# Selective-scan hybrid network: the order of VectorE's product with C and the next side step in a unit

## The chip, the cores and the metric

The kernel runs on one NeuronCore of a Trainium2 chip. The metric is device time in microseconds (us) of one execution, the median of several runs. The engines are named as in the profile: PE (TensorE, matrix multiplications), DVE (VectorE), ACT (ScalarE), POOL (GpSimd), SP (SyncE, which here only issues DMAs).

## The reference

The input is an image batch x of shape (4, 96, 64, 64). Four layers follow each other: a selective scan over the image in four directions (layer 0), a convolution block (layer 1), a spectral block with a feed-forward part (layer 2), and an attention product with a feed-forward part (layer 3). The change touches only the scan of layer 0. Cut to it, for each image and each of the four directions k:

```
xs     = the image's 192 channels after convolution and SiLU, as a sequence of 4096 places
B, C   = 16 values each per place;  delta = softplus(...) per channel and place
h[l]   = exp(delta[l] * A) * h[l-1] + (delta[l] * xs[l]) * B[l]       # 192 channels x 16 states
y[l]   = sum over the 16 states of h[l] * C[l]
```

The y of the four directions are turned back, added, normalised over the channels and multiplied by a weight. The output has the input's shape.

## The kernel before, in words

**Units.** One batch image, one direction and one stretch of 1024 places make a step. A step has 24 units: each holds 32 channels x 4 states on 128 partitions, with 1024 places along the free axis. There are 1536 units in all. `scans` runs them one after the other in an order written out by hand; the compiler's scheduler does not reorder its instructions (it stands under `manual_schedule`). One turn of its loop is a slot.

**What one unit issues**, with the lines of the profile:

- `inputs` (L1280, POOL): w = (delta * x) * B, two slots ahead.
- `decays` (L1287, ACT): da = exp(delta * A) into a pair of PSUM banks, one slot ahead. There are two such pairs, so the decay of unit s+2 goes into the banks that unit s has used. Just before it, `keep` (L1315, ACT) copies the last state of unit s for the step that follows it.
- `states` (L1303, DVE): the scan. If the unit's product goes to POOL, the scan writes over w in SBUF; if it goes to DVE, the scan writes over da in PSUM.
- `product` (L1318): w = h * C, either on DVE, issued right behind the scan, or on POOL, issued two slots later. `share` decides which, from a running estimate of how far DVE is ahead of POOL: 860 products go to DVE and 676 to POOL.
- `sums` (L1341, PE): the sum over the states by matmuls into `ps_y`, three slots behind the second unit of a pair.

**Side work.** All other layers run beside the scan. Each is a generator that yields one small step at a time with its engine and an estimated time: `pe(...)`, `ac(...)` or `dv(...)`. At the end of each slot the loop calls `advance` until a budget (`owed`) is spent or nothing fits. A step that changes the engine is, as a rule, only taken in a later slot than the step before it. A DVE step adds its estimated time to `beside[0]`, which is then added to `ahead_by[0]`, the estimate that `share` reads. So DVE's queue holds, slot by slot: the scan, its product if it is DVE's, and the DVE side steps of that slot.

DVE side steps that this text names: L633 and L636 (the softplus of delta and the product delta * x; L636 reads what L633 wrote), L755 and L757 (output normalisation and residual), L849 (residual of the convolution block), L894, L896 and L912 (layer norm and a cast of layers 2 and 3).

**Buffers.** Four tiles each of delta, delta * x, B and C, eight of w; their loads are issued by SP at fixed units of a step.

The end of a slot, before:

```
            if x is not None:
                states(x)
            for group in due.get(slot, ()):
                sums(group)
            ...
            while owed > 0.0:
                did = advance(stages)
                if did is None:
                    break
                owed -= did
                ahead_by[0] += beside[0]
                beside[0] = 0.0
```

Of the kernel before, what the change touches and what calls it, by code (L numbers as in the profile page):

```python
# [97 lines left out]
def hybrid_kernel(ctx: ExitStack, tc: tile.TileContext, a: dict):  # L98
# [4 lines left out]
    nc = tc.nc  # L103
# [352 lines left out]
    def flush():  # L456
        while to_store:
            out, t, then = to_store.pop(0)
            store(out, t)
            if then is not None:  # L460
                then()
# [763 lines left out]
    def plan():  # L1225

        stats = (group_norm(b, arriving(b)) for b in range(1, B))
        out = [Stage("weights", 2, later_weights(), *stats)] + front(1) + front(2)
        out += middle(0) + layers_2_and_3(0) + front(3)
        for b in (1, 2):  # L1230
            out += middle(b) + layers_2_and_3(b)
        return out

    def scans(stages):
# [22 lines left out]
        def fetch(step, name, i):  # L1257
            t = step[name][i] = wide(name)
            if name in "BC":
                lo = 4 * i + (NS if name == "C" else 0)  # L1260
                of = d_bc[step["k"]][step["b"] % 3][step["c"], lo : lo + 4].unsqueeze(0)
            else:
                of = (d_delta if name == "d" else d_du)[step["k"]][step["b"] % 3]
                of = of[step["c"], 32 * i : 32 * i + 32].unsqueeze(1)
            load(t, of.to_broadcast([32, 4, CH2]))

        def need(step):

            while not traced[step["b"]].issuperset((step["k"] % 2, 2 * step["c"] + e) for e in (0, 1)):
                force(stages)  # L1270
            flush()
# [6 lines left out]
        def inputs(x):  # L1278
            x["w"] = wide("w")
            nc.gpsimd.tensor_mul(x["w"], x["step"]["g"][x["i"]], x["step"]["B"][x["j"]])  # L1280

        def decays(x, last):
            if last is not None:
                keep(last)
            av = (x["step"]["k"] * NI + x["i"]) * NJ + x["j"]
            x["da"] = decay_banks()
            act(x["da"], x["step"]["d"][x["i"]], AF.Exp, scale=aneg[:, av : av + 1])  # L1287

        def share(x):

            on_vector, on_pool = PRODUCT_US
            lead = ahead_by[0] + SCAN_US - on_pool
            x["pool"] = abs(lead - on_pool) < abs(lead + on_vector)
            lead += -on_pool if x["pool"] else on_vector
            ahead_by[0] = max(-AHEAD, min(lead, AHEAD))

        def states(x):
            step, u = x["step"], x["u"]
            share(x)
            order = slice(None, None, -1) if step["k"] >= 2 else slice(None)  # L1300
            x["h"] = x["w"] if x["pool"] else x["da"]
            start = 0.0 if step["n"] == 0 else steps[x["number"] - 1]["last"][:, u : u + 1]
            nc.vector.tensor_tensor_scan(  # L1303
                x["h"][:, order], x["da"][:, order], x["w"][:, order], start, ALU.mult, ALU.add
            )
            if not x["pool"]:
                product(x, nc.vector)

        def keep(x):
            step, u = x["step"], x["u"]  # L1310
# [6 lines left out]
        def product(x, engine):  # L1317
            x["made"] = engine.tensor_mul(x["w"], x["h"], x["step"]["C"][x["j"]])  # L1318
# [12 lines left out]
        def sums(group):  # L1331
            step, first, last = group[0]["step"], group[0]["j"] == 0, group[0]["j"] == NJ - 1
            if first:
                step["y"] = bank("y")
            y = step["y"]

            made = None
            for m in (1, 0):
                for e in (1, 0):
                    q = 2 * e + m  # L1340
                    done = mm(y[32 * q : 32 * q + 32], lhsT=const("stack"), rhs=group[m]["w"][:, e * CH : e * CH + CH],  # L1341
                              start=first, stop=last)
                    if made is None:
                        made = group[0]["made"]
                        tc.add_manual_dep(done.ins, made.ins.name, mybir.DependencyInfo(
                            mybir.DependencyClass.Sync, mybir.DependencyReason.DATA), reason="sums")
            if last:
                summed.append((group, y))

        def sums_out():  # L1350
            while summed:
                group, y = summed.pop(0)
                step = group[0]["step"]
                yt = sp.tile([128, CH], F32, name="yt", bufs=1)
                nc.scalar.copy(yt, y)
                which = group[0]["pass"]
                for e in (0, 1):
                    to = d_y[step["k"]][step["b"] % 2][2 * step["c"] + e]
                    later(to[64 * which : 64 * which + 64], yt[64 * e : 64 * e + 64],
                          (lambda b=step["b"]: through(b)) if which == len(PASSES) - 1 and e == 1 else None)  # L1360

        owed = 0.0
        stages += plan()
        behind = middle(B - 1)
        stages += behind
# [7 lines left out]
        for slot in range(len(units) + 6):  # L1373
            clock[0] = slot
            x = units[slot] if slot < len(units) else None
            if x is not None:
                if x["u"] == 0:


                    last = len(units) - NST * PC  # L1380
                    if slot < last:
                        rate = max(RATE, sum(s.work for s in stages if s not in behind) / (last - slot))
                    else:
                        rate = sum(s.work for s in stages) / (len(units) - slot)
                for name, i in OWN.get(x["u"], ()):
                    fetch(x["step"], name, i)
                if x["number"] + 1 < len(steps) and x["u"] in LOADS:
                    if x["u"] == 14:
                        need(steps[x["number"] + 1])
                    for name, i in LOADS[x["u"]]:  # L1390
                        fetch(steps[x["number"] + 1], name, i)
            flush()
            if slot + 1 < len(units):
                decays(units[slot + 1], units[slot - 1] if slot > 0 else None)
            sums_out()
            if slot + 2 < len(units):
                inputs(units[slot + 2])
            if 2 <= slot < len(units) + 2 and units[slot - 2]["pool"]:
                product(units[slot - 2], nc.gpsimd)
# [4 lines that stand above are left out]
            for e, (us, most) in SHARE.items():  # L1404
                room[e] = min(room[e] + us, most)
            tensor[0] = 0.0
            held_banks[0] -= freed[0]
            freed[0] = 0
            owed = min(owed + rate, 8.0)
            while owed > 0.0:  # L1410
                did = advance(stages)
                if did is None:
                    break
                owed -= did
                ahead_by[0] += beside[0]
                beside[0] = 0.0
        flush()


    clock, tensor = [-1], [0.0]  # L1420
    beside, ahead_by = [0.0], [0.0]
# [45 lines left out]
    def advance(stages):  # L1467

        while stages and not stages[0].fill():
            stages.pop(0)  # L1470
        if stages:
            banks_left = BANKS["mm"] - held_banks[0]
            for stream in stages[0].active:
                engine, us, banks, _ = stream["next"]
                if banks and banks > banks_left:

                    banks_left = 0
                elif fits(stream):
                    if engine != "wait":
                        room[engine] -= us  # L1480
                    if engine == "pe":
                        tensor[0] += us
                    if engine == "dve":
                        beside[0] += us
                    return stages[0].step(stream)
        return None
# [21 lines left out]
    with tc.manual_schedule(engines={nc.tensor.engine, nc.scalar.engine, nc.vector.engine, nc.gpsimd.engine, nc.sync.engine}):  # L1508
        scans(stages)
# [153 lines left out]
```

## Time and profile before

| what | value |
|---|---|
| median of 3 runs | 6039.0 us (6030.13 to 6051.08) |
| the profiled execution | 6029.4 us; span of its instructions 6027.6 us |
| granted PE clock in it, mean | 0.857 |
| busy: DVE / POOL / ACT / PE | 88% / 86% / 64% / 76% of the span |
| scans on DVE (L1303) | 1536, about 2.34 us each |
| products with C on DVE (L1318) | 860, 1.225 us each |
| products with C on POOL (L1318) | 676, 2.375 us each |
| decays on ACT (L1287) | 1536, 1.116 us each |
| last scan starts / last product on DVE starts | 5545.7 / 5544.6 us |

How to read the lines: a group line gives the source line, the engine, the operation, output <- inputs, the shapes and the count; then the busy time in us and the mean of one in ns; then the idle time of the engine just before these instructions and what ended most of it. A wait line gives who waited for whom, with the total in us, the number of times and the longest. A timeline line gives start and duration in us. The scan phase runs from about 100 us to 5548 us; after it only the last image's layers 1 to 3 remain.

### The profile page before, as it was taken

The numbers are of one execution on the slowest core, as the hardware profiler recorded it, in microseconds if no ns is written. First come the engines' busy times: TensorE is split into PE (matmuls) and PEld (weight loads), VectorE is DVE, ScalarE is ACT, GpSimd is POOL, SyncE is SP. The second block draws the span as 40 slices with busy tenths as digits, with TensorE's granted clock in tenths as the row PEclk, the third lists the DMA queues.
The fourth block names the chain that finished last, engine by engine and source line by source line (L and its number), as shares of the span: only waits on it lengthen the run. The fifth ranks groups of instructions, "written<-read, shape, count | busy, mean of one in ns | idle before, by whom it ended". The sixth has DMA issues, their size and how long they took to land. (4 is left out here: it accounts for less than half of the span.)

```text
span 6027.6 us, 78329 instructions
## 1 busy us (share of the span) xinstructions
PE 4564.8 (76%) x27668; PEld 1682.2 (28%) x27668; DVE 5280.0 (88%) x3583; ACT 3856.1 (64%) x6056; POOL 5154.5 (86%) x2219
## 2 busy tenths in 40 slices
PE   6743867755898776686568888768888877779998
PEld 2100212211222642121012246211222642112284
DVE  4999898899999899989999999999999999897045
ACT  4853776764665677877556657777666677665335
POOL 4987898999999999989999999999999999897000
PEclk9855978877999888797689989878999888789999
DMA  5654575667754654466776446557754664674101
GB/s 182 229 177 152 195 227 183 219 211 232 216 161 148 200 194 154 159 196 205 229 238 186 164 159 217 166 175 224 220 173 155 199 199 144 184 239 146 48 16 38
DMA packets 425084, 1078.44 MB, mean 179 GB/s; under 512 B 79378, under 2 KB 81268, under 8 KB 423540
## 3 DMA queue, kind: packets, MB, share of 16 engines
q1 hardware_dynamic: 424692, 1073.44, 56.0%
q8 instruction: 219, 3.59, 0.3%
q14 instruction: 173, 1.42, 0.1%
HBM read 857.02 MB, written 220.66 MB: 179 GB/s over the span
## 5 line engine op out<-in xcount | busy, mean ns | idle before, releaser
L1280 POOL TENSOR_TENSOR scan_w<-scan_g,scan_B 128x1024 f32<-128x1024 f32 x1536 | 3606.5, 2376 | 242.0 <-PE ps_y L1341 112.3
L1287 ACT ACTIVATE ps_da<-scan_d,aneg 128x1024 f32<-128x1024 f32 x1536 | 1714.4, 1116 | 324.3 <-DVE scan_w L1318 176.1
L1318 POOL TENSOR_TENSOR scan_w<-scan_w,scan_C 128x1024 f32<-128x1024 f32 x676 | 1605.4, 2375 | 153.3 <-ACT state L1315 102.4
L1303 DVE TENSOR_TENSOR_SCAN ps_da<-ps_da,state,scan_w 128x1024 f32<-128x1024 f32 x633 | 1483.0, 2343 | 103.8 <-ACT ps_da L1287 92.5
L1341 PE MATMUL ps_y<-scan_w,cst 128*32 128x512 f32 x6144 | 1003.0, 730 | 590.8 <-POOL scan_w L1318 297.8
L1303 DVE TENSOR_TENSOR_SCAN scan_w<-ps_da,state,scan_w 128x1024 f32<-128x1024 f32 x519 | 1214.2, 2341 | 32.9 <-ACT ps_da L1287 30.7
L1318 DVE TENSOR_TENSOR scan_w<-ps_da,scan_C 128x1024 f32<-128x1024 f32 x860 | 1053.1, 1225 | 71.7 <-DMA scan_C<-bc 6.4
L1303 DVE TENSOR_TENSOR_SCAN ps_da<-ps_da,scan_w 128x1024 f32<-128x1024 f32 x227 | 518.4, 2284 | 58.3 <-ACT ps_da L1287 51.1
L1341 PEld LDWEIGHTS ps_y<-scan_w,cst 128*32 128x32 f32 x6144 | 147.2, 117 | 1221.5 <-POOL scan_w L1318 505.1
L1315 ACT COPY state<-ps_da 128x1 f32<-128x1 f32 x654 | 104.1, 159 | 488.4 <-DVE scan_w L1318 486.5
L829 PE MATMUL ps_mm<-h,wd 128*32 128x512 f32 x3144 | 363.5, 593 | 7.0 <-ACT r L169 7.0
L1303 DVE TENSOR_TENSOR_SCAN scan_w<-ps_da,scan_w 128x1024 f32<-128x1024 f32 x157 | 357.8, 2279 | 9.5 <-ACT ps_da L1287 6.9
L567 PE MATMUL ps_mm<-xp,taps 128*128 128x512 f32 x576 | 285.9, 639 | 51.6 <-ACT xp L547 22.2
L806 PE MATMUL ps_mm<-wd,w 128*32 128x512 f32 x1944 | 243.1, 613 | 17.9 <-ACT h L810 8.7
L618 PE MATMUL ps_mm<-xd,dtw 128*128 128x512 f32 x256 | 165.4, 737 | 70.8 <-ACT z L640 43.8
L1315 ACT COPY state<-scan_w 128x1 f32<-128x1 f32 x498 | 93.2, 187 | 192.0 <-DVE scan_w L1303 191.6
L627 ACT ACTIVATE z<-ps_mm 128x512 f32<-128x512 f32 x192 | 114.4, 596 | 148.3 <-PE ps_mm L622 76.5
L633 DVE SCALAR_TENSOR_TENSOR ps_mm<-ps_mm,z 128x512 f32<-128x512 f32 x192 | 131.3, 684 | 87.7 <-ACT z L631 82.6
L888 PE MATMUL ps_mm<-r,cst 128*128 128x512 f32 x220 | 149.4, 768 | 62.4 <-ACT r L885 13.8
L672 PE MATMUL ps_mm<-ya,cst 128*64 128x512 f32 x192 | 183.2, 1043 | 9.1 <-ACT acc L912 8.6
L810 ACT ACTIVATE h<-ps_mm 128x512 f32<-128x512 f32 x258 | 150.6, 596 | 53.8 <-PE ps_mm L806 50.9
L829 PEld LDWEIGHTS ps_mm<-h,wd 128*32 128x32 f32 x3144 | 110.6, 109 | 239.8 <-issue 207.3
(360 smaller groups left out, 6536.9 us busy)
## 6 DMA issues: line engine op xcount, KB each, us to landing
scan_g<-du SPq DMA_DIRECT2D x384, 512.0 KB, 5.0
scan_d<-delta SPq DMA_DIRECT2D x384, 512.0 KB, 5.9
scan_B<-bc SPq DMA_DIRECT2D x256, 512.0 KB, 5.3
scan_C<-bc SPq DMA_DIRECT2D x256, 512.0 KB, 5.2
y<-yt SPq DMA_DIRECT2D x384, 128.0 KB, 2.7
du<-g SPq DMA_DIRECT2D x128, 256.0 KB, 3.0
delta<-z SPq DMA_DIRECT2D x128, 256.0 KB, 2.8
tab<-in_etab SPq DMA_DIRECT2D x112, 256.0 KB, 4.0
```

The source lines that it names most:

```text
L567: mm(p, lhsT=taps[:, t, 0:128], rhs=window(t, c + e), start=t == 0, stop=t == 8)
L618: mm(p, lhsT=dtw[:, o + 2 * third, 0:128], rhs=xd, start=True, stop=True)
L672: mm(split(p[:64]), lhsT=const("two")[:, :64], rhs=t[:, :L].rearrange("p (w h) -> p h w", h=H)[:, c * RPC : (c + 1) * RPC, :], start=True, ...
L806: mm(p[32 * n : 32 * n + 32], lhsT=w1[:, 32 * g : 32 * g + 32], rhs=xin[:, n : n + 15 : 2, 1 : W + 1], start=True, stop=True)
L810: act(h[:, :, 1 : W + 1], split(p), AF.Relu)
L829: mm(p[32 * n : 32 * n + 32], lhsT=held["wd"][:, groups[i], o, dx, :], rhs=here[i][:, :, dx : dx + W], start=dx == 0, stop=dx == 2)
L1280: nc.gpsimd.tensor_mul(x["w"], x["step"]["g"][x["i"]], x["step"]["B"][x["j"]])
L1287: act(x["da"], x["step"]["d"][x["i"]], AF.Exp, scale=aneg[:, av : av + 1])
L1303: nc.vector.tensor_tensor_scan(x["h"][:, order], x["da"][:, order], x["w"][:, order], start, ALU.mult, ALU.add)
L1315: nc.scalar.copy(step["last"][:, u : u + 1], x["h"][:, end : end + 1])
L1318: x["made"] = engine.tensor_mul(x["w"], x["h"], x["step"]["C"][x["j"]])
L1341: done = mm(y[32 * q : 32 * q + 32], lhsT=const("stack"), rhs=group[m]["w"][:, e * CH : e * CH + CH], start=first, stop=last)
```

## The change

A product that belongs to DVE is no longer issued in `states`. The unit is put into a list, `waiting`. It is taken out, and the product issued, behind the first call of `advance` in the slot that issued DVE work; where no call does, behind the last one. The functions `states` and the loop of `scans` change, and a function `multiply` is new.

```
                 x["h"][:, order], x["da"][:, order], x["w"][:, order], start, ALU.mult, ALU.add
             )
             if not x["pool"]:
-                product(x, nc.vector)
+                waiting.append(x)
+
+        def multiply():
+            while waiting:
+                product(waiting.pop(0), nc.vector)
 
...
-        owed = 0.0
+        owed, waiting = 0.0, []
...
                 if did is None:
                     break
                 owed -= did
+                if beside[0]:
+                    multiply()
                 ahead_by[0] += beside[0]
                 beside[0] = 0.0
+            multiply()
         flush()
```

The new lines shift those below: the product with C is L1322 in the changed kernel, the state copy L1319, the sums L1345; L1303, L1287 and L1280 keep their numbers.

## The prediction

> **What bounds the kernel now.** I read the busy times of the page first, then one long window of the scan phase, then VectorE's (DVE's) groups with shapes kept apart, then the waits of VectorE and ScalarE (ACT), and last the timeline at two places where the change acts.
>
> ```profile
> PE 4564.8 (76%) x27668; PEld 1682.2 (28%) x27668; DVE 5280.0 (88%) x3583; ACT 3856.1 (64%) x6056; POOL 5154.5 (86%) x2219
> ```
> ```profile
> core 0: us, PE busy (x) PEld busy (x) DVE busy (x) ACT busy (x) POOL busy (x), PEclk, DMA share, GB/s
> 1000.00:5500.00 4500.00, 3457.10 (x21266) 1251.30 (x21263) 4225.59 (x2640) 3023.14 (x4745) 4303.77 (x1853) 0.86 0.61 192
> ```
> In the scan phase VectorE is busy 4225.59 / 4500 = 94% and GpSimd (POOL) 96%. Both are near full; neither alone is the bound. ScalarE is at 67%.
>
> ```profile
> L1303 DVE TENSOR_TENSOR_SCAN ps_da<-ps_da,state,scan_w 128x1024 f32<-128x1024 f32 x633 | 1483.0, 2343 | 103.8 <-ACT ps_da L1287 92.5 <-POOL scan_w L1280 5.6 <-ACT state L1315 4.0
> L1318 DVE TENSOR_TENSOR scan_w<-ps_da,scan_C 128x1024 f32<-128x1024 f32 x860 | 1053.1, 1225 | 71.7 <-DMA scan_C<-bc 6.4 <-DVE ps_da L1303 0.9 <-PE ps_mm L672 0.4
> L633 DVE SCALAR_TENSOR_TENSOR ps_mm<-ps_mm,z 128x512 f32<-128x512 f32 x192 | 131.3, 684 | 87.7 <-ACT z L631 82.6 <-ACT state L1315 5.1
> ```
> The product with C (L1318) runs 860 times on VectorE, 1225 ns each. Of the 71.7 us of idle time before it only 6.4 + 0.9 + 0.4 have a named cause; 64 us, 74 ns per product, do not. The next rows show what that is.
>
> ```profile
> 862.90 2.35 DVE L1303 TENSOR_TENSOR_SCAN ps_da<-ps_da,state,scan_w 128x1024 f32<-128x1024 f32 x1
> 865.28 1.22 DVE L1318 TENSOR_TENSOR scan_w<-ps_da,scan_C 128x1024 f32<-128x1024 f32 x1
> 866.42 0.69 DVE L633 SCALAR_TENSOR_TENSOR ps_mm<-ps_mm,z 128x512 f32<-128x512 f32 x1
> 867.14 1.03 DVE L636 TENSOR_TENSOR g<-ps_mm,ub 128x512 f32<-128x512 f32 x1
> 868.09 2.35 DVE L1303 TENSOR_TENSOR_SCAN scan_w<-ps_da,state,scan_w 128x1024 f32<-128x1024 f32 x1
> ```
> Start plus duration against the next start: the scan ends at 865.25 and its product, which reads what it wrote, starts 0.03 us later (in other places 0.09 to 0.10). L633, which needs nothing of the product, starts 0.08 us *before* the product's record ends. L636, which reads L633's output, starts 0.03 after it. The next scan starts 0.08 before L636 ends. So on this engine a dependent follower starts 0.03 to 0.10 us after its predecessor's end and an independent one 0.08 before.
>
> ```profile
> DVE ps_da L1303 <- ACT ps_da L1287: 143.6, 114, 5.4
> DVE ps_mm L633 <- ACT z L631: 82.6, 25, 31.8
> POOL scan_w L1318 <- ACT state L1315: 102.4, 78, 6.6
> ACT state L1315 <- DVE scan_w L1318: 486.5, 297, 11.0
> ACT ps_da L1287 <- DVE scan_w L1318: 176.1, 100, 5.1
> ```
> VectorE's own waits are mostly for ScalarE, above all for the decay (L1287). ScalarE in turn waits 486.5 + 176.1 us for the product: the state copy of a unit, or the decay that takes the same pair of PSUM banks two units on, stands behind that unit's product. The product has a follower.
>
> **The change, part by part.** Nothing is removed or added: 1536 scans, 860 products on VectorE and 676 on GpSimd, and the same side steps. The choice between the engines (share) sees the same numbers. In the built order PE, ScalarE, GpSimd and SyncE keep their order; no DMA and no transfer moves. Only VectorE's order differs. In 626 of the 860 units no VectorE side step follows in the unit, and the product stands where it stood. In 234 it moves behind one (221 of them behind a single instruction): 71 behind L633, 30 behind L896, 27 behind L912, 22 behind L755, 18 behind the first L849, 17 behind L894, the other 49 behind smaller ones.
>
> *Saved, scan to product.* Over these 234 the timeline's gap from scan to product averages +70 ns; behind an independent instruction it is -83. So 153 ns x 234 = 36 us.
>
> *Saved inside the side step.* In 71 units the product now stands between L633 and L636, in 22 between L755 and L757. Both pairs are dependent (+35 ns before, -83 with the product between them): 118 ns x 93 = 11 us. Together 47 us.
>
> Here a rule stands against the change. The Trainium skill ("VectorE: DVE Perf Modes", section "The DRAIN you can't avoid") says that after every VectorE operation the next one doesn't start until the pipe is empty, and that chaining operations with or without semaphores took the same time. By it the order of independent instructions saves nothing: 0 instead of 47 us. The rows above differ (-0.08 against +0.03 to +0.10, over hundreds of pairs), and the measurement decides: I take 47.
>
> *Lost, the side step not ready.* The moved side instruction now comes up one product earlier, 1.3 us. I took for each of the 234 the time at which the last thing it waits for (a ScalarE, PE or DMA event in the trace) was there. For 184 it was there before the scan ended: no stall, and these alone make -36 us of the 47. For 50 it was not: VectorE would stand 76 us with the product ready behind it, of which 32 us were idle already after the product. New: 44 us. The worst are L633 (16 of 71), L894 (7 of 17) and L755 (15 of 22), as here:
>
> ```profile
> 1582.40 2.36 DVE L1303 TENSOR_TENSOR_SCAN ps_da<-ps_da,state,scan_w 128x1024 f32<-128x1024 f32 x1 [0.15 <-ACT ps_da L1287]
> 1584.86 1.23 DVE L1318 TENSOR_TENSOR scan_w<-ps_da,scan_C 128x1024 f32<-128x1024 f32 x1
> 1584.93 1.02 PE L753 MATMUL ps_mm<-yrow,wc_b 128*96 128x512 f32 x2
> 1586.06 0.69 DVE L755 TENSOR_TENSOR ps_mm<-sq,ps_mm 96x512 f32<-96x512 f32 x1
> 1586.79 0.75 DVE L757 SCALAR_TENSOR_TENSOR xc<-ps_mm,wout_bias,xc 96x512 f32<-96x512 f32 x1
> ```
> L753's matmul ends at 1585.95, just before L755 starts: today the product covers that wait exactly. Put behind L755, VectorE stands from 1584.7 to 1586.06 and the product ends near 1587.9 instead of 1586.09.
>
> *On VectorE alone:* -47 + 44 = -3 us.
>
> *The follower.* The moved product ends later by 0.48 us in the middle case (one side instruction). Queued behind it on ScalarE are that unit's state copy (0.2 us), the decay two units on (1.12), and the evictions of the side steps. Put against ScalarE's records, 134 of the 234 would start that copy later, by 92 us in sum. Between the product and the scan that needs the decay lies a whole scan of 2.35 us against 0.2 + 1.12 on ScalarE; with all other times kept, in none of the 134 does the decay come too late. So it is first costed at nothing, hidden by the next unit's scan. If that cover is gone because ScalarE is itself behind, it costs up to 92 us. Where is ScalarE the one that paces? 168 of 1536 scans (11%) waited for their decay. 92 x 0.11 = 10 us, an estimate.
>
> *Others that could wait for the product.* The sums (L1341) run three units later and wait for GpSimd's product, made two units late, far more than for this one; 0.5 us of VectorE's does not reach them. The C tile is read by GpSimd two units later too, so its reload does not move. GpSimd at 96% could swallow a gain, but has 196 us of idle time in the window's 4500, several times 47.
>
> *Sum:* -47 + 44 + 10 = +7 us on the profiled execution's 6029.4 (span 6027.6, 1.8 around it), 6036. That execution lies at the low end of the runs (6030.13 to 6051.08), 9.6 below their median 6039.0, so on the median 6046.
>
> Both ends of the unknowns: the stalls cost 76 - 32 = 44 at most and nothing if other idle time behind them takes them up; the follower 0 to 92; the saving 0 (by the rule) to 47.
>
> **The rivals.** About 0.3%, 18 us, is what a measurement of this kernel can tell from no change.
>
> *ScalarE restarts late (slower).* The place: the state copy L1315 behind a product that itself stands behind a side step that waits for ScalarE or PE. VectorE then waits for ScalarE's z or r while ScalarE's next decay waits for VectorE's product; in series, where they ran beside each other. For it: ScalarE already waits 662 us for this product, and L633 82.6 us for z. Against it: the 2.35 us scan in between. It decides from (18 + 3) / 92 = 23% of the late 92 us reaching a scan; at 40% it is -3 + 37 = +34, 6073, and at all of it +89, 6128. The skill's rule, if it held, would land on the same side, at +44.
>
> *The stalls fold into idle time that is there (faster).* VectorE has 274 us of idle time in the window's 4500. If a stalled side step only takes the place of the next wait for a decay, much of the 44 vanishes, while the 184 unstalled places keep their 36: 6039 - 36 = 6003; with all 47, 5992. For it: where PE or ScalarE is late, a wait for the decay often follows. Against it: where a wait follows anyway, a saved 0.15 us only lengthens it.
>
> *It does nothing.* 73% of the products do not move, and GpSimd at 96% may set the pace: 6039. That lies inside my forecast's band.
>
> **How the numbers follow.** The forecast (gain and stalls cancel, a little lost on ScalarE) gets 0.44; most of its spread is within 18 us (0.31), 0.08 above, 0.05 below. The late restart gets 0.32, nearly all slower (0.31). The folded stalls get 0.24, nearly all faster (0.22), 0.02 within. Faster 0.05 + 0.22 = 0.27; same 0.31 + 0.01 + 0.02 = 0.34; slower 0.08 + 0.31 = 0.39. The likeliest single case is the first, 6046; its own range is 6025 to 6062. The 8-in-10 range reaches down to the faster rival's 6003 and up to 6105, two thirds of the slower one's reach.
>
> **What would show it.** Right: the product's idle time falls from 71.7 us to below 45 with no cause named; "DVE ps_mm L633 <- ACT z L631" grows from 82.6 by 10 to 20 us, and L755 and L894, with 1.0 us of idle time from PE L753 and 28.9 from r, grow by some 10 each; the state copy's wait for L1318 grows from 486.5 by tens of us; the idle time of L1303 for L1287 (143.6 + 37.7) changes by less than 20. Wrong: if the product's unnamed idle time stays near 64 us, the drain is not saved by order. If L1303's wait for L1287 grows by 30 us or more, the late restart has won. If the waits of L633, L755 and L894 stay as they are, the stalls were folded.

## The result, and the profile after

| | median us | range | ratio to before, 95% interval |
|---|---|---|---|
| before | 6040.03 (4 runs) | 6030.13 to 6051.08 | |
| changed | 5999.76 (4 runs) | 5997.25 to 6012.37 | 0.9943 (0.993 to 0.9957) |

The changed kernel is faster by 0.57%, some 34 us (26 to 42). The ratio comes from the single runs of both kernels and is not the quotient of the two medians, which is 0.9933; the same holds for all ratios below. I had forecast 6046 us, no clear change with a lean to slower; the time lies 3 us below the range, at the place of the rival "the stalls fold into idle time that is there" (6003).

Page of the changed kernel, busy times, and its window of the scan phase:

```profile
PE 4565.3 (76%) x27668; PEld 1684.2 (28%) x27668; DVE 5246.4 (87%) x3583; ACT 3853.7 (64%) x6056; POOL 5152.9 (86%) x2219
```
```profile
1000.00:5500.00 4500.00, 3484.88 (x21394) 1262.17 (x21396) 4222.43 (x2653) 3038.03 (x4765) 4325.75 (x1864) 0.86 0.60 192
```
The same number of VectorE instructions took 5246.4 us and not 5280.0: 33.6 us less busy time. Records that overlap count once, and now more of them overlap: worked out from both traces, the overlap of VectorE's records grew by 29.8 us, and the sum of their durations fell by only 3.8. The fixed window holds 13 more VectorE instructions and 11 more of GpSimd.

VectorE's groups of the changed kernel (the product is L1322 now):

```profile
L1303 DVE TENSOR_TENSOR_SCAN ps_da<-ps_da,state,scan_w 128x1024 f32<-128x1024 f32 x633 | 1483.2, 2343 | 105.3 <-ACT ps_da L1287 93.5 <-POOL scan_w L1280 4.4 <-ACT state L1319 3.9
L1322 DVE TENSOR_TENSOR scan_w<-ps_da,scan_C 128x1024 f32<-128x1024 f32 x860 | 1050.1, 1221 | 55.3 <-DMA scan_C<-bc 6.7 <-DVE ps_da L1303 0.9
L633 DVE SCALAR_TENSOR_TENSOR ps_mm<-ps_mm,z 128x512 f32<-128x512 f32 x192 | 130.6, 680 | 95.9 <-ACT z L631 92.0 <-ACT state L1319 3.7
```
The product's idle time fell from 71.7 to 55.3 us. Together with the busy time that is 33.6 + 16.4 = 50 us saved. The two places of the prediction, in the changed kernel's timeline (start, duration, both in us):

```profile
861.14 2.35 DVE L1303 TENSOR_TENSOR_SCAN ps_da<-ps_da,state,scan_w 128x1024 f32<-128x1024 f32 x1
863.40 0.67 DVE L633 SCALAR_TENSOR_TENSOR ps_mm<-ps_mm,z 128x512 f32<-128x512 f32 x1
863.99 1.21 DVE L1322 TENSOR_TENSOR scan_w<-ps_da,scan_C 128x1024 f32<-128x1024 f32 x1
865.12 1.03 DVE L636 TENSOR_TENSOR g<-ps_mm,ub 128x512 f32<-128x512 f32 x1
...
1575.10 2.33 DVE L1303 TENSOR_TENSOR_SCAN ps_da<-ps_da,state,scan_w 128x1024 f32<-128x1024 f32 x1
1578.59 0.69 DVE L755 TENSOR_TENSOR ps_mm<-sq,ps_mm 96x512 f32<-96x512 f32 x1 [1.16 <-PE ps_mm L753]
1579.19 1.21 DVE L1322 TENSOR_TENSOR scan_w<-ps_da,scan_C 128x1024 f32<-128x1024 f32 x1
1580.33 0.74 DVE L757 SCALAR_TENSOR_TENSOR xc<-ps_mm,wout_bias,xc 96x512 f32<-96x512 f32 x1
```
In the first, each of the three starts about 0.08 us before its predecessor ends: scan, side step, product and second side step run without a gap. In the second, VectorE stands 1.16 us for the matmul with the product ready behind it, as foreseen. The waits of VectorE and ScalarE:

```profile
DVE ps_da L1303 <- ACT ps_da L1287: 145.5, 111, 7.0
DVE ps_mm L633 <- ACT z L631: 92.0, 30, 31.9
DVE scan_w L1303 <- ACT ps_da L1287: 29.0, 35, 2.8
DVE ps_mm L755 <- PE ps_mm L753: 11.8, 15, 1.7
ACT state L1319 <- DVE scan_w L1322: 547.0, 331, 11.2
ACT ps_da L1287 <- DVE scan_w L1322: 207.3, 103, 12.6
```
The stalls are there: L633 +9.4 us, L755 +10.8, L894 +4.0 (28.9 to 32.9), and some 7 more at L896, L912 and L518; about 32 us in all. The follower is there too: ScalarE waits 754.3 us for the product and not 662.6, 92 us more. Yet the scans wait less for their decay, 174.5 us (145.5 + 29.0) and not 181.3. Of that sum before, 143.6 stands in the prediction and the rest in this line:

```profile
DVE scan_w L1303 <- ACT ps_da L1287: 37.7, 54, 3.8
```
Sum on VectorE for the profiled executions: busy -33.6; idle +5.7 (stalls +32, product -16, scans of all forms -8, the rest -2); span -27.9. This is bookkeeping of one execution each: busy and idle time always add up to the span, so it does not tell what a microsecond of any of these terms costs the kernel. The experiments ask that.

### The profile page after: what moved, and what is told of

It is laid out like the page before. It is cut to its first block, busy times and chain, and to the rows that moved or that the text cites. A ratio compares the mean times of both kernels' runs of the same rounds, so it can differ in the third digit from the quotient of the medians.

```text
span 5999.7 us, 78283 instructions
## 1 busy us (share of the span) xinstructions
PE 4565.3 (76%) x27668; PEld 1684.2 (28%) x27668; DVE 5246.4 (87%) x3583; ACT 3853.7 (64%) x6056; POOL 5152.9 (86%) x2219
## 5 line engine op out<-in xcount | busy, mean ns | idle before, releaser
L1280 POOL TENSOR_TENSOR scan_w<-scan_g,scan_B 128x1024 f32<-128x1024 f32 x1536 | 3605.8, 2376 | 222.1 <-PE ps_y L1345 94.7
L1287 ACT ACTIVATE ps_da<-scan_d,aneg 128x1024 f32<-128x1024 f32 x1536 | 1714.4, 1116 | 331.5 <-DVE scan_w L1322 207.3
L1322 POOL TENSOR_TENSOR scan_w<-scan_w,scan_C 128x1024 f32<-128x1024 f32 x676 | 1605.4, 2375 | 148.9 <-ACT state L1319 98.6
L1303 DVE TENSOR_TENSOR_SCAN ps_da<-ps_da,state,scan_w 128x1024 f32<-128x1024 f32 x633 | 1483.2, 2343 | 105.3 <-ACT ps_da L1287 93.5
L1345 PE MATMUL ps_y<-scan_w,cst 128*32 128x512 f32 x6144 | 1003.8, 731 | 622.4 <-POOL scan_w L1322 317.5
L1303 DVE TENSOR_TENSOR_SCAN scan_w<-ps_da,state,scan_w 128x1024 f32<-128x1024 f32 x519 | 1213.9, 2340 | 25.9 <-ACT ps_da L1287 23.8
L1322 DVE TENSOR_TENSOR scan_w<-ps_da,scan_C 128x1024 f32<-128x1024 f32 x860 | 1050.1, 1221 | 55.3 <-DMA scan_C<-bc 6.7
L1303 DVE TENSOR_TENSOR_SCAN ps_da<-ps_da,scan_w 128x1024 f32<-128x1024 f32 x227 | 518.4, 2284 | 57.9 <-ACT ps_da L1287 52.0
L1345 PEld LDWEIGHTS ps_y<-scan_w,cst 128*32 128x32 f32 x6144 | 146.5, 117 | 1246.0 <-POOL scan_w L1322 522.9
L1319 ACT COPY state<-ps_da 128x1 f32<-128x1 f32 x654 | 104.2, 159 | 548.6 <-DVE scan_w L1322 547.0
L1303 DVE TENSOR_TENSOR_SCAN scan_w<-ps_da,scan_w 128x1024 f32<-128x1024 f32 x157 | 357.7, 2279 | 7.7 <-ACT ps_da L1287 5.3
L633 DVE SCALAR_TENSOR_TENSOR ps_mm<-ps_mm,z 128x512 f32<-128x512 f32 x192 | 130.6, 680 | 95.9 <-ACT z L631 92.0
L1319 ACT COPY state<-scan_w 128x1 f32<-128x1 f32 x498 | 93.3, 187 | 169.9 <-DVE scan_w L1303 169.5
```

The lines of the kernel that those rows point to most:

```text
L1303: nc.vector.tensor_tensor_scan(x["h"][:, order], x["da"][:, order], x["w"][:, order], start, ALU.mult, ALU.add)
L1319: nc.scalar.copy(step["last"][:, u : u + 1], x["h"][:, end : end + 1])
```

## The experiments

Ratios are to the kernel before, run on the same chip; 0.001 is 6 us.

**Which places pay (e1, e2).** The product moves only in the units of a list; elsewhere it stays right behind its scan. e1 holds the 184 units whose side step was ready in the trace of before, e2 the 50 others.

```
             if not x["pool"]:
-                waiting.append(x)
+                if clock[0] in BEHIND:
+                    waiting.append(x)
+                else:
+                    product(x, nc.vector)
```

> The product is moved behind the side step only in the 184 units (by number) in which the trace of before had that side step's inputs there before the scan ended; in the other 50 it stays right behind its scan. Theory K (the prediction's book: saving 47 us, new stalls 44 us, each landing in full): these 184 alone give -36 us, ratio 0.994, and more than the whole change. Theory F (the stalls fold into idle time that VectorE has anyway): 184/234 of the change's gain, -25 to -30 us, 0.995 to 0.996, a little less than the whole change. Theory N (the gain is no saving at all but another alignment of the engines): no relation to the part that is kept.

> The complement: the product is moved only in the 50 units in which the side step was not ready at the scan's end. Theory K: the new stalls of 44 us less these units' share of the saving, 10 us: +33 us, ratio 1.0055. Theory F: stalls fold, only the share of the saving is left, -10 to 0 us, 0.998 to 1.000. The prediction's follower (ScalarE restarts late) would add to K's side, up to 1.007.

Measured: e1 0.9948 (0.9934 to 0.9963), 6003.14 us; e2 0.9999 (0.9989 to 1.0008), 6036.51 us. Before, three of the four waits that matter (the fourth, L633's 82.6, stands in the prediction; L755's is in its group line):

```profile
DVE xp L896 <- ACT r L170: 64.6, 13, 11.5
DVE xq L894 <- ACT r L170: 28.9, 17, 4.9
L755 DVE TENSOR_TENSOR ps_mm<-sq,ps_mm 96x512 f32<-96x512 f32 x30 | 20.4, 680 | 1.0 <-PE ps_mm L753 1.0
```
VectorE's waits in e2:

```profile
DVE ps_mm L633 <- ACT z L631: 96.6, 29, 31.7
DVE xp L896 <- ACT r L170: 69.7, 19, 11.5
DVE xq L894 <- ACT r L170: 34.3, 19, 4.9
DVE ps_mm L755 <- PE ps_mm L753: 8.9, 14, 1.0
```
and in e1:

```profile
DVE ps_mm L633 <- ACT z L631: 82.9, 26, 33.1
DVE xp L896 <- ACT r L170: 63.5, 12, 11.5
DVE xq L894 <- ACT r L170: 29.2, 15, 4.9
```
So the list was right about which places stall: in e2 these four waits are 32 us above before (82.6, 64.6, 28.9, 1.0), in e1 the three shown are as before. But the time doesn't follow. e2's +33 did not come; its upper bound is +5 us. These 50 places also save their share, about 10 us on VectorE, which e3 and e10 below make worth 4 to 5 us; so the 32 us of stalls may have cost some 5 us, and hardly more than 10. And e1 alone keeps 31 of the 34 us: the changed kernel, with the stalls in it, is not told apart from e1 without them (to some 12 us either way). Theory K, the prediction's book, falls: a stall seen on VectorE is mostly not a microsecond of the kernel.

**The saving without the order (e3).** The order of before; in the same 234 units 192 columns of VectorE's product are left out.

```
-            x["made"] = engine.tensor_mul(x["w"], x["h"], x["step"]["C"][x["j"]])
+            n = CH2 - 192 if engine is nc.vector and clock[0] in SHORT else CH2
+            x["made"] = engine.tensor_mul(x["w"][:, :n], x["h"][:, :n], x["step"]["C"][x["j"]][:, :n])
```

> The order of before, unchanged; in the 234 units that the change moves, VectorE's product covers 832 of its 1024 columns (the last 192 are left unmultiplied, so that part of the scan's sum is left out), which takes about 0.2 us each, 47 us in sum, from VectorE: the change's saving with no side step earlier and no product later. Theory K with the follower: VectorE's time counts in full and the moved order costs 44 + 10 on top, so without that cost -40 to -47 us, 0.992 to 0.9935, clearly below the changed kernel. Theory F: the moved order costs little, so this is near the changed kernel, -32 to -42 us, 0.993 to 0.995. Theory G (GpSimd at 96% sets the pace): under -20 us, above 0.9965.

Measured: 0.9969 (0.9958 to 0.998), 6019.16 us. The group of the shortened products:

```profile
L1334 DVE TENSOR_TENSOR scan_w<-ps_da,scan_C 128x832 f32<-128x832 f32 x234 | 239.8, 1025 | 16.4
```
234 x (1225 - 1025) ns = 47 us were taken, and 19 us (12 to 25) came out: 0.4 us for each. That is far below the ranges of K and F. It lies in the range of theory G, but G's reason does not hold: e8 below takes time from GpSimd itself and finds a tenth of a microsecond for one.

**The order without the saving (e5, e9), and more work alone (e6, e10).** Behind each of the 234 products a small operation that nobody reads spends the 47 us again; e5 and e9 on the changed order, e6 and e10 on the order of before. First with a multiplication:

```
+            if engine is nc.vector and clock[0] in MOVED:
+                c = x["step"]["C"][x["j"]][:, :120]
+                engine.tensor_mul(spin, c, c)
```

> The changed kernel's order; behind each of the 234 moved products VectorE runs one more small, independent multiplication (128x120, read by nobody), about 0.2 us each with the overlap, so that the 47 us that the order saves on VectorE are spent again. What is left is the order itself: side steps 1.3 us earlier, products later. Theory S (besides the saved time, the side step's result comes earlier, and PE and ScalarE wait less for it): a gain is left, about -15 us, the 34 of the change less the 19 of the saving alone, 0.997 to 0.998. Theory A (all of the change's gain is the saved time, the saving alone was only measured low): nothing is left, 0.999 to 1.001. Follower (late restart of ScalarE): a loss is left, 1.001 to 1.003.

> The order of before; the same small multiplication behind the product of the same 234 units: 47 us more work on VectorE, no order changed. It measures what a microsecond of VectorE is worth, from the other side. If it is worth 0.4 us, as the saving alone says (-19 of 47): +19 us, 1.003. Theory A: +35 to +47 us, 1.006 to 1.008. If idle time takes it up: under +6 us, below 1.001.

Measured: 1.0298 and 1.0387. The spender was a failure. The tile's view in e6:

```profile
L1337 DVE TENSOR_TENSOR spin<-scan_C x234: 271/1334/8146, 119.0 to 5749.8; 128x120 f32<-128x120 f32 x117
```
Minimum, median and maximum in ns: instead of 0.28 us each it took 1.43 in the mean (below), so some 315 us were added and not 47 (the last section shows why). Then with one SBUF input:

```
+            if engine is nc.vector and clock[0] in MOVED:
+                nc.vector.bn_stats(spin, x["step"]["C"][x["j"]][:, :120])
```

> As e5, with a spender that can't meet GpSimd: behind each of the 234 moved products one bn_stats over 120 columns of the C tile (one SBUF input, read by nobody; 512 columns take 0.68 us at L518), about 0.2 us with the overlap. The 47 saved us are spent again. Theory S (the earlier side steps are a gain of their own): -10 to -20 us, 0.997 to 0.998. Theory A (the change is worth its saved time and no more): 0.999 to 1.001. Follower: 1.001 to 1.003.

> The order of before with the same bn_stats behind the product in the same 234 units: 47 us more on VectorE, nothing else. A microsecond of VectorE worth 0.4 us (as the saving alone said): 1.003; worth 0.7 (as e5 and e6 say, 208 of about 300 us and 234 of 315): +33 us, 1.0055; worth 1: 1.008.

Measured: e9 0.9983 (0.9973 to 0.9993), 6025.57 us; e10 1.0038 (1.0024 to 1.0052), 6057.52 us. The same view in e10:

```profile
L1336 DVE BATCH_NORM_STATS2 spin<-scan_C x234: 274/275/278, 118.8 to 5549.1; 128x6 f32<-128x120 f32 x117
```
With the 0.08 us of overlap that is 0.19 us x 234 = 45 us added, for 23 us (14 to 31) of time: 0.5 us for each. So from both sides a microsecond of VectorE is worth about half of one at this size. And the order alone, all stalls and late products in it and nearly nothing saved (some 5 of the 50 us are left unspent, worth 2 to 3), is a gain of 10 us (4 to 16). Theory S said 10 to 20. The two parts, -19 and -10, add up to -29 against -34 measured, which agrees within their intervals.

**A later product (e4).** The call of `multiply` inside the loop is left out; the product comes at the end of its slot.

```
-                if beside[0]:
-                    multiply()
```

> The product is put behind all VectorE side steps of its slot and not behind the first: the same 234 units, but the product is late by 1.04 us in the mean and not by about 0.5, and the pairs L633-L636 and L755-L757 stand together again (11 us of the saving lost). Theory F: only those 11 us are lost, about -25 us, 0.996. The follower (ScalarE restarts late): twice the lateness, so some 92 us more of late restarts on ScalarE; with even a fifth of it reaching a scan -5 us or above, 0.999 to 1.003.

Measured: 0.9986 (0.9977 to 0.9996), 6026.93 us, some 26 us above the changed kernel. Its waits of ScalarE:

```profile
ACT state L1319 <- DVE scan_w L1322: 620.6, 349, 11.3
ACT ps_da L1287 <- DVE scan_w L1322: 237.1, 110, 14.4
```
and the scans' waits for their decay:

```profile
DVE ps_da L1303 <- ACT ps_da L1287: 137.9, 114, 7.1
DVE scan_w L1303 <- ACT ps_da L1287: 28.3, 33, 4.5
```
ScalarE's wait for the product is 195 us above before, against the change's 92. The 11 us of pairs that stand together again account for 5 us at half value; about 20 (10 to 30) are left. Two things differ besides: the product is later, and the second side step is earlier. A follower that costs at twice the lateness would fit, but the trace does not show its path: the scans wait 166.2 us for their decay, less than in the changed kernel (174.5). This execution, span 6010.0, lies 15 us below its kernel's median, so it may miss what made the others longer. The cause of the 20 us stays open.

**Is GpSimd a pace too, and is the split right (e8, e7, e11)?** e8 leaves 88 columns out of 234 of GpSimd's products, in the order of before; e7 and e11 are the changed kernel with another estimate in `share`.

```
+            n = CH2
+            if engine is nc.gpsimd:
+                pooled[0] += 1
+                if pooled[0] * 234 // 676 > (pooled[0] - 1) * 234 // 676:
+                    n = CH2 - 88
```
```
-SCAN_US, PRODUCT_US = 2.35, (1.2, 2.37)
+SCAN_US, PRODUCT_US = 2.32, (1.2, 2.37)      # e7; e11: 2.38
```

> The order of before; in 234 of the 676 products on GpSimd, evenly spread, 936 of the 1024 columns are multiplied (88 columns left out, that part of the sum is missing), about 0.2 us each, 47 us in sum, taken from GpSimd. Two paces: a microsecond of GpSimd is worth as much as one of VectorE, -15 to -25 us, 0.996 to 0.9975. If VectorE alone paces: 0 to -5 us, above 0.999. If GpSimd is the pace (and VectorE's 0.4 is what is left for it): -30 us or more, below 0.995.

> The changed kernel with the scan's estimate in share at 2.32 us and not 2.35 (the 47 saved us spread over 1536 units are 0.03 each): 873 products go to VectorE and not 860, 217 of them behind a side step and not 234. GpSimd is relieved of 13 x 2.375 = 31 us, VectorE gets some 16 us more and loses 17 moved places, 3 us. Theory two paces (VectorE and GpSimd, at 94% and 96%, both set the time): -5 to -10 us against the changed kernel, 0.992 to 0.9935. If VectorE alone paces: +8 to +16 us against it, 0.9955 to 0.997.

> The changed kernel with the scan's estimate at 2.38 us: 847 products on VectorE and not 860, 222 of them behind a side step. The opposite of e7. VectorE alone paces (GpSimd's 45 us were worth about nothing in e8): VectorE loses 16 us of work and 12 moved places, 2 us: -6 to -14 us against the changed kernel, 0.992 to 0.9935. If the split was at its best for both engines: slower than the changed kernel by 5 to 15 us, 0.995 to 0.997.

Measured: e8 0.9992 (0.9983 to 1.0), e7 0.9987 (0.9978 to 0.9995), e11 0.9958 (0.9941 to 0.9974). The two forms of GpSimd's product in e8:

```profile
L1325 POOL TENSOR_TENSOR scan_w<-scan_w,scan_C 128x1024 f32<-128x1024 f32 x442 | 1049.3, 2374 | 121.9 <-ACT state L1317 75.2 <-DVE scan_w L1305 37.1 <-PE ps_y L1348 6.8
L1325 POOL TENSOR_TENSOR scan_w<-scan_w,scan_C 128x936 f32<-128x936 f32 x234 | 510.5, 2182 | 38.5 <-ACT state L1317 21.0 <-DVE scan_w L1305 14.4 <-DVE sd L177 2.6
```
2182 ns in the place of 2374 are 45 us less on GpSimd, and 5 us (0 to 10) came out. Busy 96% of the time before, GpSimd is worth about a tenth of a microsecond for one here. Neither other split beat the change: e7 is 26 us above it, slower than both of its expectations allowed, and e11, expected 6 to 14 us below the change if VectorE alone paces, is not told apart from it.

**More places (e12).** A bias in `share`: where a VectorE side step can be taken in this slot, the product rather goes to VectorE.

```
+            beneath = any(s["next"][0] == "dve" and fits(s) for s in stages[0].active) if stages else False
+            seen = lead - 1.0 if beneath else lead + 0.5
-            x["pool"] = abs(lead - on_pool) < abs(lead + on_vector)
+            x["pool"] = abs(seen - on_pool) < abs(seen + on_vector)
```

> The changed kernel with a bias in share: where a VectorE side step is ready to be taken in this slot, the product goes to VectorE rather than GpSimd (by 1.0 us of lead), elsewhere rather to GpSimd (by 0.5). The split stays (861 on VectorE), but 312 of them stand behind a side step and not 234. Theory A: 78 places x 0.2 us = 16 us more saved on VectorE, worth 6 to 11 us: 0.9925 to 0.993. Theory K (each late side step costs in full, the folding was the particular 50 places'): no better than the changed kernel, 0.994 to 0.996. A rougher alternation of the two engines could cost more: above 0.997.

Measured: 0.9976 (0.9965 to 0.9987), 6019.51 us: 20 us worse than the change, with 312 places and not 234. VectorE was busy 5234.0 us, 12 less than in the changed kernel; GpSimd stood longer before its input products:

```profile
POOL scan_w L1280 <- PE ps_y L1347: 139.1, 76, 7.0
```
In the changed kernel:

```profile
POOL scan_w L1280 <- PE ps_y L1345: 94.7, 59, 5.7
```
Theories A and K are both missed. The last choice in the expectation, a rougher alternation, fits; by itself it was not tried.

**Does the gain belong to one alternation (e13 to e16)?** Both kernels with `share`'s estimate started at 1.5 us (e13 before, e14 changed) and at 3.0 (e15, e16): the same work, other units on VectorE.

```
-    beside, ahead_by = [0.0], [0.0]
+    beside, ahead_by = [0.0], [1.5]      # e15, e16: [3.0]
```

> The kernel before, with share's running estimate started at 1.5 us and not 0: 860 products on VectorE as before, the same work, but which units they are differs. If the alternation as such makes little difference: 0.999 to 1.001. If it alone makes +-20 us (as e7 and e12 leave possible): 0.9965 to 0.999 or 1.001 to 1.0035.

> The changed kernel with the same start of 1.5 us: 860 products on VectorE, 235 of them behind a side step. Theory M (the change gains by its mechanism: 0.2 us saved in each of about 234 places, late side steps fold): the same gain against e13 as the change against before, 0.9935 to 0.996 of e13. Theory N (the gain belongs to that one alternation of units): anything, 0.998 to 1.002 of e13 among it.

> As e13 with a start of 3.0 us: 859 products on VectorE, other units again. Alternation makes little difference: 0.999 to 1.001; it makes +-20 us: outside that.

> The changed kernel with the start of 3.0 us: 859 products on VectorE, 220 behind a side step. Theory M: 0.994 to 0.9965 of e15, a little less than the change, for 220 places. Theory N: no fixed relation to e15.

| start of the estimate | before's order, us | changed order, us | changed / before |
|---|---|---|---|
| 0 | 6040.03 | 5999.76 | 0.9943 |
| 1.5 | 6026.56 (e13, 0.9993) | 5991.58 (e14, 0.994) | 0.9947 |
| 3.0 | 6049.31 (e15, 1.0031) | 6026.62 (e16, 0.9986) | 0.9955 |

The last column is worked out from the ratios to before. The gain is there three times out of three and in theory M's ranges, so theory N falls. But the alternation alone moves the time by up to 0.3%. So the 20 to 26 us by which e7 and e12 fell behind can't be put down to their edits; they also changed the alternation. e1 to e4 and e8 to e10 keep it.

e14 has the lowest median of all kernels, 5991.58 us (0.994, 0.9926 to 0.9954); its interval overlaps the changed kernel's, so it is as good and not shown better.

**What no run separates: the granted PE clock.** Among runs of one and the same kernel, those with a lower granted clock are longer. The 24 runs of the kernel before that go with e9 to e12 reach from 6021.0 us at 0.861 to 6050.6 us at 0.852, about 2.5 us for each 0.001 by a straight line through them. The kernels differ in it too. The changed kernel has 0.8575 in the mean of its four runs and e9 0.858, against 0.856 to 0.857 for before; e10 has 0.853; in the last two rows of the table the changed order is above before's by 0.004 and 0.005. If the clock were a cause of its own, 3 to 4 of the change's 34 us, some 10 of e10's 23 us and 3 of e9's 10 would be its share, and some 9 of 32 and 12 of 27 us in those two rows; a microsecond of VectorE would then be worth nearer 0.3 than 0.5. All of these would keep their sign. It can as well be that the order of the work sets the clock. No run here decides that.

## Why the prediction was wrong, and where it was right

- **Saved, 47 us on VectorE: right in size.** 50 us measured (16.4 of idle time, 29.8 of overlap, 3.8 of shorter records). I had quoted a rule of the Trainium skill against it ("VectorE: DVE Perf Modes", section "The DRAIN you can't avoid"), and left out its exception: the same section adds that a next operation which isn't held starts earlier. The rows of independent pairs (-0.08 us) agree with that; whether they are "held" in the page's sense was not worked out. One sign was set wrong: the product's idle time was to fall below 45 us. Only the 70 ns of gap are idle time; the 83 ns of overlap show in the busy sum.
- **Saved time counted at par: wrong.** I took a microsecond of VectorE as one of the kernel. It is worth 0.4 (e3) to 0.5 (e10). This error alone would have made the forecast slower still.
- **New stalls, 44 us, each landing in full: the step that failed.** 32 us of them showed on VectorE, at the lines I named. On the clock they cost some 5 us, hardly more than 10 (e2). I wrote that the cost lay between nothing and 44 and took the upper end, though VectorE had 274 us of idle time in the window. Between ends so far apart, and with a named rival to fold them, the upper end was the wrong choice. My sign for the folding was wrong as well: the waits of L633, L755 and L894 were to stay as they are, but they grew, and still the time did not.
- **The follower, +10 us: no cost seen at this lateness.** ScalarE waited 92 us longer for the product. I had worked out 92 us too, but for the state copies alone, whose wait grew by 60.5; the other 31.2 are the decays' wait, so that the two figures agree is luck. In sum the scans did not wait longer for their decay (174.5 us against 181.3). That the scan in between hides it fits, and was not tested by itself.
- **Not seen: the order itself is a gain.** The side step is 1.3 us earlier, and with nearly all of the saved time spent again this leaves -10 us (e9). PE's wait for the residual, before, changed, and e9:

```profile
PEld ps_mm L882 <- DVE o L849: 69.3, 14, 7.0
PEld ps_mm L882 <- DVE o L849: 56.8, 13, 7.0
PEld ps_mm L882 <- DVE o L849: 58.6, 13, 6.9
```
It fell by 11 to 13 us, which fits. But in e3, where no order changed, it fell too, to 61.8 us; so what makes the order's gain stays open.
- **The rivals.** The faster one had the time, 6003, and was right that the stalls hardly cost. Its number is in part luck: it counted the saving of 36 us at par; in truth half the saving and the order's own gain make up the sum. "It does nothing" falls with the result, and its reason, that GpSimd sets the pace, with e8.

So the term of the sum that was mis-sized is the price of a stall and of a delay: +44 and +10, +54 in my sum. The order with all its stalls and late products, and the saved time spent again, measured -10 (e9).

## What to carry to other kernels

In this kernel two dependent VectorE instructions in a row left a gap of 0.03 to 0.10 us, and an independent instruction between them filled it: look for start-to-end gaps that have no named cause, and put work there. A saving on an engine that was 94% busy was worth half of its length or less, and a stall less still, in a kernel where several engines hand work to each other: put a price on it by taking away or adding a known amount at the same places before any sum of microseconds is trusted. And before a difference of 0.3% is explained, run the same edit on another, equally good arrangement of the same work.

## What the runs showed of the hardware

- **A VectorE operation with two SBUF inputs waits for GpSimd.** The 128x120 multiplication of e6, both inputs in SBUF, took 271 ns at best and 1428 in the mean beside a GpSimd whose multiplications take 2.4 us; the bn_stats of e10, one SBUF input of the same size, took 274 to 278 ns, and the product (one input in PSUM) 1223 to 1227 ns before the change. Worked out from the traces: of the 234 in e6, 193 took over 0.4 us, and every one of them ended 0.137 to 0.147 us after the end of a GpSimd instruction; in e5 it is 206 of 234, with the same two bounds. The longest of e6:

```profile
5595.23 2.40 POOL L1334 TENSOR_TENSOR scan_w<-scan_w,scan_C 128x1024 f32<-128x1024 f32 x1
5596.51 8.15 DVE L1337 TENSOR_TENSOR spin<-scan_C 128x120 f32<-128x120 f32 x1
5597.53 6.99 POOL L1296 TENSOR_TENSOR scan_w<-scan_g,scan_B 128x1024 f32<-128x1024 f32 x3
```
The Trainium skill ("SBUF — State Buffer", section "Who interferes with whom") says that such an instruction contends with a GpSimd instruction that reads SBUF, and that the second waits for the whole of the first. The traces agree, and show more: this one waited for the rest of one GpSimd instruction and for three more that followed without a gap; in e6, 15 of the 234 waited through two to four. I had overlooked the page when I made the spender.

- **A follower's start on VectorE.** 0.08 us before its predecessor's record ends where it is independent (median of the 626 pairs of a product and the next scan before the change: -0.083), 0.03 to 0.10 after where it reads what that one wrote (856 pairs of a scan and its product before the change, median 0.091).
